# Gated cross-attention with RMS norm: the next quad's scores behind the last attention products of the quad before

## The chip, the cores and the metric

One core of a Trainium2 chip runs the kernel. The metric is the time of one execution on the device in microseconds (us), as the median of several runs. Five engines work side by side, each through its own queue: TensorE (PE in the profile, its weight loads PEld), VectorE (DVE), ScalarE (ACT), GpSimd (POOL) and SyncE (SP), which here only issues DMAs.

## The reference

```python
memory_proj = einsum('bme,de->bmd', memory, W_mem)
scores = einsum('bnd,bmd->bnm', hidden_states, memory_proj) / sqrt(D)
attn = softmax(scores, axis=-1)
memory_context = einsum('bnm,bmd->bnd', attn, memory_proj)
gate_input = concatenate([hidden_states, memory_context], axis=-1)
gate = sigmoid(einsum('bnf,df->bnd', gate_input, W_gate) + b_gate)
fused = hidden_states + gate * memory_context
return fused * rsqrt(mean(fused ** 2, axis=-1) + 1e-6) * norm_w
```

hidden_states (x) is 8 x 1024 x 1024, memory is 8 x 64 x 512, W_mem is 1024 x 512, W_gate is 1024 x 2048, all in float32.

## The kernel before

**Preparation.** Up to some 84 us the kernel projects the memory, multiplies the projection with the second half of W_gate, so that the context's part of the gate becomes attn times a small matrix (mg), and prepares sums of the blocks of W_gate's first half. Then come 16 **quads** of 512 rows of x, two to a batch (QPB is 2).

**The gate's large product.** Each quad multiplies x (512 x 1024) with the first half of W_gate (1024 x 1024) by Strassen's method in Winograd's form, on two levels. The outer level has seven products, done in the order 1, 6, 7, 5, 4, 2, 3 (ORDER, line 527). Their left sides are the transposed blocks of x (tiles a11, a12, a21, a22) and outer sums of these, S1 to S4 (outer_s, line 254; S3 overwrites a21 and S4 uses S2 and a12). Each outer product is again split into seven small ones, which the code names A, B, C, D, A again, E, F (outer_product, line 669): two matmuls each, 128x256 out, in float32, which the profile shows as four matmul records. Their left sides are quarters of the outer left side or the inner sums s1 to s4 (inner_s, line 283), which GpSimd makes in two parts: s1 and s2 first, then s3 and s4. B uses s2, C uses s3, D uses s1, F uses s4. A to F land in PSUM banks of which there are five; VectorE adds them up (u2, u3, u4 and the sums in fin), and GpSimd adds u's into the output tiles ahead of that (pre).

**The order of work** is written out by hand. Every small product is one **slot**; a quad has 49, and t0 is its first. at(slot, fn) places an operation just before the small product of that slot, mid((q, o), fn) places it in outer product o of quad q, between the second A and E. plan(q), line 530, fills both for one quad. All engines take what is queued in program order.

**Attention.** In slot 7 (before A of product 6) scores(q) multiplies the transposed x with the projected memory: 16 matmuls (k = 0..7, r = 0, 1), 64 columns wide, so that two run side by side in halves of the array (128*64 in the profile), into psT; ScalarE copies it to sT (line 309). Slot 9 transposes it on TensorE (sc), slots 10 and 13 do the softmax on VectorE and ScalarE, slot 18 transposes the result (pa, line 342), ScalarE copies it to attnT. Outer products 5, 4, 2 and 3 then carry attention's products between the second A and E: eight matmuls of 64 rows, again two side by side (64*128), half of them into pc (the context), half into the banks A, F, E, D (the gate's second part).

**x.** load_xq(q + 1) in slot 2 loads the next quad's x into a single buffer; transpose_x makes the blocks of A on VectorE, 128x512 at a time: rows 2 and 3 beside products 5 and 2, rows 0 and 1 in slots 36, 38, 43 and 45. Outer sums 1 and 2 of the next quad stand beside product 3, outer sums 3 and 4 in slot 7. Outer sum 3 overwrites a21, which scores reads.

**mg and the bias.** For a new batch load_mg loads mg in slot 49, which is slot 0 of the next quad, once attention's products of product 3 have read the old one. add_bias (line 371) then adds b_gate to its second half by an accumulating DMA on GpSimd's queue, in slot 8.

**Behind the gate.** sigmoid on ScalarE, gated on VectorE (times pc), the residual x by an accumulating DMA on GpSimd's queue, square on ScalarE and norm on VectorE, which for the second half of a quad's rows fall into slots 3 to 14 of the next quad.

Of the kernel before, what the change touches and what calls it, by code (L numbers as in the profile page):

```python
# [20 lines left out]
def tile_gated_cross_attention_rmsnorm(  # L21
# [46 lines left out]
    QPB = N // QT  # L68
# [31 lines left out]
    def t4k(pool, shape, tag, name):  # L100
        return pool.tile(shape, F32, tag=tag, name=name)
# [33 lines left out]
    for k in range(KD):  # L135
        t = t4k(*((gpool, [P, D], "gate") if k < 7 else (apool, [P, D], "s4")), f"w2_{k}")
# [383 lines left out]
    def at(slot, fn, *args):  # L520
        due.setdefault(slot, []).append(lambda: fn(*args))

    def mid(key, fn, *args):
        beside.setdefault(key, []).append(lambda: fn(*args))
# [5 lines left out]
    def plan(q):  # L530
        t0 = SLOTS * q
        nxt = q + 1 < NQ
        order = [o for o, _ in ORDER]
        for i, o in enumerate(order):
            for part, t in ((0, 1), (1, 5)):
                if i + 1 < len(order):
                    at(t0 + 7 * i + t, inner_s, q, order[i + 1], part)
                elif nxt:
                    at(t0 + 7 * i + t, inner_s, q + 1, order[0], part)
        at(t0 + 7, scores, q)  # L540
        at(t0 + 7, outer_s, q, 3)
        at(t0 + 7, outer_s, q, 4)
        at(t0 + 9, transpose_scores, q)
        at(t0 + 10, softmax_a, q)
        at(t0 + 13, softmax_b, q)
        at(t0 + 18, transpose_attn, q)
        at(t0 + 21, attn_difference, q)
        if not nxt:
            at(t0 + 5, load_last)
            return  # L550
        at(t0 + 2, load_xq, q + 1)
        for t in (2, 3):
            mid((q, 5), transpose_x, q + 1, t, 0)
            mid((q, 2), transpose_x, q + 1, t, 1)
        for i, t, half in ((36, 0, 0), (38, 1, 0), (43, 0, 1), (45, 1, 1)):
            at(t0 + i, transpose_x, q + 1, t, half)
        mid((q, 3), outer_s, q + 1, 1)
        mid((q, 3), outer_s, q + 1, 2)
        if (q + 1) % QPB == 0:
            at(t0 + 10, load_mp, (q + 1) // QPB)  # L560
            at(t0 + 49, load_mg, (q + 1) // QPB)
        if q % QPB == 0:
            at(t0 + 8, add_bias, q // QPB)

    for o in (2, 3):
        w1_place(o)
# [246 lines left out]
    for q in range(NQ):  # L813
        plan(q)
        for o, ext in ORDER:
            outer_product(q, o, ext)
# [29 lines left out]
```

## Time and profile before

| | |
|---|---|
| median of 3 runs | 980.95 us (980.92 to 981.3) |
| profiled span | 979.4 us |
| granted TensorE clock, mean | 0.996 |
| TensorE busy | 964.8 us |
| VectorE busy | 820.4 us |
| GpSimd busy | 730.5 us |
| ScalarE busy | 324.9 us |
| scores (psT), 16 blocks of 32 matmul records | 58.8 us |
| start of the scores in quads 7 and 8 | 421.00 and 476.05 us |

How to read the lines that follow: a row of the timeline holds the start in us, the duration in us, the engine, the line of the code, the operation, "written<-read" by the program's names with buffer numbers left out, the shape, and how many instructions were merged. In brackets stands how long the engine was idle just before, and what released it. Matmuls are pipelined, so their durations overlap: what counts is the distance from one start to the next. A row of the waits has engine and operation, what it waited for, the sum in us, how often and the longest. "issue" is time in which the engine waited for nothing that the profile shows. Names: kA to kF are the small products, u and gate are VectorE's and GpSimd's sums of them, l is the tile of inner sums, a and s are the left sides.

### The profile page before, as it was taken

What the parts mean: (1) busy time and instruction counts of PE and PEld (TensorE: products, weight loads), DVE (VectorE), ACT (ScalarE), POOL (GpSimd) and SP (SyncE); (2) the same over time, 40 slices, a digit from 0 to 9 for tenths busy, and PEclk for the clock granted to TensorE, in tenths of its full rate; (3) what the DMA queues carried; (4) which work ended last, traced back from release to release, by engine and by line L of the source; (5) the groups of instructions that cost most, each with busy time, mean ns of one, the idle gap of its engine ahead of it and who ended that gap; (6) DMA issues with size and microseconds to landing.
All of it is one profiled execution on the core that took longest, in us unless ns stands there. A gap on an engine that the chain in (4) does not pass through costs nothing.

```text
span 979.4 us, 14277 instructions
## 1 busy us (share of the span) xinstructions
PE 964.8 (99%) x4938; PEld 769.8 (79%) x4938; DVE 820.4 (84%) x1487; ACT 324.9 (33%) x602; POOL 730.5 (75%) x881
## 2 busy tenths in 40 slices
PE   9999999999999999999999999999999999999995
PEld 6546888888887888888887888888887888888873
DVE  3888788979797988979797988979797988979787
ACT  1100234151433334151433334151433334151434
POOL 3366877878787877878787877878787877878772
PEclk9999999999999999999999999999999999999998
DMA  9865264482918374482918374482818364482612
GB/s 372 258 153 145 39 120 107 103 188 62 186 65 165 108 141 106 102 190 65 183 65 164 111 138 105 107 184 66 182 65 168 110 136 104 108 184 68 169 65 86
DMA packets 71255, 128.32 MB, mean 131 GB/s; under 512 B 12432, under 2 KB 49296, under 8 KB 70928
## 3 DMA queue, kind: packets, MB, share of 16 engines
q1 hardware_dynamic: 61760, 93.34, 35.3%
q0 software_dynamic: 9280, 33.56, 18.5%
q8 instruction: 39, 0.64, 0.3%
q10 hardware_dynamic: 144, 0.52, 0.2%
q14 instruction: 32, 0.26, 0.1%
HBM read 87.56 MB, written 39.85 MB: 130 GB/s over the span
## 4 chain that ended last, share of the span: by engine, by line
PE 96%; DVE 2%; DMA 1%; issue 0%; ACT 0%; POOL 0%; DVEq 0%; ACTq 0%
PE kA L92 20%; PE pc L92 12%; PE kE L92 11%; PE kF L92 10%; PE kD L92 10%; PE kC L92 10%; PE kB L92 10%; PE psT L92 6%; PE pg L92 5%; PE pm L92 3%; DVE gate L95 1%; DMA memq<-in_mem 1%; DVE gate L660 0%; PE pa L342 0%; PE sc L316 0%
## 5 line engine op out<-in xcount | busy, mean ns | idle before, releaser
L95 POOL TENSOR_TENSOR gate<-gate,u 128x256 f32<-128x256 f32 x336 | 270.4, 835 | 115.7 <-DVE u L95 110.1
L582 ACT ACTIVATE gate<-gate 128x512 f32<-128x512 f32 x128 | 79.0, 629 | 400.1 <-DVE gate L95 400.1
L95 POOL TENSOR_TENSOR l<-a 128x256 f32<-128x256 f32 x128 | 128.9, 1007 | 60.4 <-DVE a L95 55.8
L248 DVE STREAM_TRANSPOSE a<-xq 128x512 f32<-128x512 f32 x128 | 137.9, 1098 | 4.0 <-DMA xq<-in_x 4.0
L92 PE MATMUL pc<-mg,attnT 64*128 64x256 f32 x512 | 127.4, 389 | 0.0
L611 DVE SCALAR_TENSOR_TENSOR gate<-gate,ss,nw_sb 128x512 f32<-128x512 f32 x120 | 126.0, 1060 | 1.1
L92 PE MATMUL kD<-it,l 128*128 128x256 f32 x448 | 115.0, 379 | 0.0
L92 PE MATMUL kB<-it,l 128*128 128x256 f32 x448 | 115.0, 379 | 0.0
L92 PEld LDWEIGHTS pc<-mg,attnT 64*128 64x128 f32 x512 | 90.6, 186 | 29.7 <-issue 21.2
L92 PE MATMUL kA<-w,a 128*128 128x256 f32 x384 | 98.7, 379 | 0.4 <-ACT u L726 0.4
L92 PEld LDWEIGHTS kD<-it,l 128*128 128x128 f32 x448 | 85.1, 190 | 11.6
L92 PEld LDWEIGHTS kB<-it,l 128*128 128x128 f32 x448 | 85.1, 190 | 11.6
L95 DVE TENSOR_TENSOR gate<-gate,pc 128x512 f32<-128x512 f32 x128 | 87.0, 680 | 5.8 <-ACT gate L582 5.8
L95 POOL TENSOR_TENSOR l<-s 128x256 f32<-128x256 f32 x96 | 75.7, 789 | 10.8 <-PE kF L92 10.7
L92 PEld LDWEIGHTS kA<-w,a 128*128 128x128 f32 x384 | 71.6, 190 | 10.2 <-ACT u L726 0.8
L726 ACT COPY u<-kA 128x256 f32<-128x256 f32 x112 | 40.5, 362 | 102.1 <-PE kA L92 99.9
L92 PE MATMUL kE<-it,a 128*128 128x256 f32 x256 | 69.0, 392 | 0.0
L95 DVE TENSOR_TENSOR u<-u,kB 128x256 f32<-128x256 f32 x112 | 45.5, 406 | 28.1 <-PE kB L92 24.9
L92 PE MATMUL kA<-t,s 128*128 128x256 f32 x256 | 67.4, 386 | 0.0
L92 PE MATMUL kC<-w,l 128*128 128x256 f32 x256 | 65.7, 379 | 0.0
L92 PE MATMUL kF<-w,l 128*128 128x256 f32 x256 | 65.7, 379 | 0.0
L596 ACT ACTIVATE junk<-gate 128x1024 f32<-128x1024 f32 x60 | 63.5, 1059 | 2.1 <-DMA gate<-in_x 1.2
(123 smaller groups left out, 1996.6 us busy)
## 6 DMA issues: line engine op xcount, KB each, us to landing
xq<-in_x SPq DMA_DIRECT2D x64, 512.0 KB, 9.6
gate<-in_x POOLq DMA_DIRECT2D x60, 512.0 KB, 7.8
out<-gate SPq DMA_DIRECT2D x60, 512.0 KB, 2.6
w<-in_w_gate_t SPq DMA_DIRECT2D x8, 512.0 KB, 11.0
w<-in_w_gate_t SPq DMA_DIRECT2D x2, 2048.0 KB, 15.6
mg<-mgd SPq DMA_DIRECT2D x16, 256.0 KB, 4.0
mpd<-mpT SPq DMA_DIRECT2D x4, 512.0 KB, 3.8
mgd<-mpq SPq DMA_DIRECT2D x16, 128.0 KB, 2.6
```

Of the source, the lines that this page charges most:

```text
L92: pin(nc.tensor.matmul(o, lhsT, rhs, start=start, stop=stop, skip_group_check=True))
L95: pin(eng.tensor_tensor(o, a, b, op))
L248: nc.vector.transpose(A[key][:, :, r * P : (r + 1) * P], chunks(xq[q][:, 4 * t : 4 * t + 4, :], KD)[:, half * KH : (half + 1) * KH],)
L582: pin(nc.scalar.activation(g, g, AF.Sigmoid))
L596: nc.scalar.activation(junk, O[q, t], AF.Square, accum_out=ss[:, t % 2 : t % 2 + 1])
L611: nc.vector.scalar_tensor_tensor(g[:, cols], g[:, cols], rstd[:, t % 2 : t % 2 + 1], nw_sb[:, cols], ALU.mult, ALU.mult,)
L726: pin(nc.scalar.copy(p1, kb["A"]))
```

## The change

Three things move; no operation is added or taken away.

1. scores(q + 1) is done at the end of quad q, beside product 3, directly behind its attention products and ahead of E, instead of in slot 7 of its own quad. Only quad 0 keeps its scores in slot 7. Attention's products and the scores, both done in parts of the array, so follow each other, and the scores' wait is out of the way of outer sum 3, which overwrites a21.
2. The last two transpositions of the next x are in slots 42 and 43 instead of 43 and 45, so that all of x is there when the scores begin.
3. The bias's DMA stands in slot 4, the fifth product of the quad, instead of slot 8; again quad 0 keeps its place.

```diff
-        at(t0 + 7, scores, q)
+        if q == 0:
+            at(t0 + 7, scores, q)
         at(t0 + 7, outer_s, q, 3)
         at(t0 + 7, outer_s, q, 4)
...
         for t in (2, 3):
             mid((q, 5), transpose_x, q + 1, t, 0)
             mid((q, 2), transpose_x, q + 1, t, 1)
-        for i, t, half in ((36, 0, 0), (38, 1, 0), (43, 0, 1), (45, 1, 1)):
+        for i, t, half in ((36, 0, 0), (38, 1, 0), (42, 0, 1), (43, 1, 1)):
             at(t0 + i, transpose_x, q + 1, t, half)
+        mid((q, 3), scores, q + 1)
         mid((q, 3), outer_s, q + 1, 1)
         mid((q, 3), outer_s, q + 1, 2)
...
         if q % QPB == 0:
-            at(t0 + 8, add_bias, q // QPB)
+            at(t0 + (4 if q else 8), add_bias, q // QPB)
```

## The prediction

> **What bounds the kernel now.** I read the page's busy line and its chain first.
>
> ```profile
> PE 964.8 (99%) x4938; PEld 769.8 (79%) x4938; DVE 820.4 (84%) x1487; ACT 324.9 (33%) x602; POOL 730.5 (75%) x881
> PE 96%; DVE 2%; DMA 1%; issue 0%; ACT 0%; POOL 0%; DVEq 0%; ACTq 0%
> ```
>
> TensorE has matmuls in flight 99% of the span and the chain lies on it for 96%. So the time falls only if TensorE gets less to do, and it rises as soon as TensorE waits. The granted clock is 0.996. Next I read one quad (the eighth) in order of time. A product slot is four matmul records and takes 0.86 us (474.23 to 475.09). Around the scores, TensorE shows:
>
> ```profile
> 474.23 1.03 PE L92 MATMUL kE<-it,a 128*128 128x256 f32 x4
> 475.09 1.03 PE L92 MATMUL kF<-w,l 128*128 128x256 f32 x4
> 476.05 3.67 PE L92 MATMUL psT<-a,mpb 128*64 128x256 f32 x32
> 479.65 1.13 PE L92 MATMUL kA<-t,s 128*128 128x256 f32 x4
> 480.62 1.03 PE L92 MATMUL kB<-it,l 128*128 128x256 f32 x4
> ```
>
> Without the scores, kF to kB would be two slots, 1.73 us; it is 5.53 us, so the scores' block costs **3.80 us**: 16 pairs at 0.216 us (0.86/4) are 3.46 us, and 0.34 us goes at its two edges. The waits of the weight loads show the same edges: psT's first load waits 5.3 us in 16 times, the first load of E behind attention's products 21.2 us in 64 times, 0.33 us each, with nothing released by another engine.
>
> Then VectorE (DVE) over the same stretch, down to product 7's u:
>
> ```profile
> 476.15 0.42 DVE L95 TENSOR_TENSOR gate<-u,kF 128x256 f32<-128x256 f32 x1 [0.44 <-PE kF L92]
> 478.04 1.23 DVE L95 TENSOR_TENSOR a<-a,a 128x1024 f32<-128x1024 f32 x1 [1.47 <-PE psT L92]
> 479.18 1.22 DVE L95 TENSOR_TENSOR s<-a,s 128x1024 f32<-128x1024 f32 x1
> 481.75 0.42 DVE L95 TENSOR_TENSOR u<-u,kB 128x256 f32<-128x256 f32 x1 [1.35 <-PE kB L92]
> 482.14 0.17 DVE L607 RECIPROCAL ss<-ss 128x2 f32<-128x2 f32 x1
> 482.34 0.75 DVE L611 SCALAR_TENSOR_TENSOR gate<-gate,ss,nw_sb 128x512 f32<-128x512 f32 x1
> ...
> 489.96 0.41 DVE L95 TENSOR_TENSOR u<-u,kB 128x256 f32<-128x256 f32 x1
> 490.48 0.42 DVE L95 TENSOR_TENSOR u<-u,kC 128x256 f32<-128x256 f32 x1
> ```
>
> DVE idles 1.47 and 1.35 us while TensorE does the scores; from 481.75 to 490.48 no row carries a wait: softmax, four norm passes of the quad before and product 6's sums fill it. Who waits for that last u is in the rows of GpSimd (POOL) and of the weight loads:
>
> ```profile
> 491.03 2.10 POOL L95 TENSOR_TENSOR gate<-gate,u 128x256 f32<-128x256 f32 x3 [1.54 <-DVE u L95]
> 493.09 0.73 POOL L95 TENSOR_TENSOR l<-s 128x256 f32<-128x256 f32 x1
> ```
> ```profile
> 492.93 0.84 PEld L92 LDWEIGHTS kB<-it,l 128*128 128x128 f32 x4
> 493.87 0.77 PEld L92 LDWEIGHTS kC<-t,l 128*128 128x128 f32 x4
> ```
>
> GpSimd starts product 7's three additions when u arrives, then makes s3 of product 5 (l<-s), finished at 493.82. TensorE's C of product 5 loads exactly that tile at 493.87, where the 0.86 cadence from 492.93 gives 493.79. Its matmul still starts on cadence (494.01 in the timeline, 0.86 behind B). The load is already held by 0.08 us, and the next microsecond of lateness lands on TensorE. So there is **a second chain without slack**: F of product 1, DVE, GpSimd, C of product 5. The quad before has 0.04 us (s3 ends at 438.71, the load is at 438.77, its cadence at 438.75).
>
> **What the Trainium skill says.** TensorEngine Tiling (Array Packing), Tiling Modes, Key Properties: changing the tiling mode drains TensorE. The trace agrees: about 0.2 us at each edge. TensorE: Matmul & The Clock Gate, "Architectural detail", says VectorE and ScalarE take instructions strictly in order; the DVE rows agree, since the outer sums behind a late instruction never overtake it. SBUF — State Buffer, "Who interferes with whom", says a VectorE instruction with two SBUF inputs and a GpSimd instruction that reads SBUF exclude each other. The trace agrees: the norm pass takes 0.75 us with GpSimd idle (482.34) and 1.05 and 1.23 us beside its additions, and the l<-a beside the second outer sum takes 1.64 us instead of 0.73.
>
> **The change part by part.**
>
> *Scores behind attention's products of product 3.* The 512 matmul records stay. Fifteen of sixteen scores blocks move. Attention's products of a product show: A to first pc 0.96 us (465.19 to 466.15), first pc to E 1.93 (to 468.08) against 8 pairs at 0.216 = 1.73, E to F 0.97. So their edges cost 0.10 + 0.20 + 0.10 = 0.40 us, the scores' 0.34; four edges, 0.74. Afterwards three are left, since the step from 64*128 to 128*64 is one edge. No row shows this step; at the least it costs an ordinary edge, 0.15 to 0.2 us (saving 0.2), at most two (saving nothing). I take 0.2, since each of the four known edges costs about that: **-0.2 us a quad**.
>
> *What the scores did where they stood.* They lay between F of product 1 and B of product 6 and gave the second chain 3.80 us, of which DVE idled 1.47 + 1.35 = 2.82. Taking them away leaves 0.98 us missing. A busy DVE starts the next instruction some 0.08 us before the recorded end of the last (u<-u,kB at 490.48 is an exception, it reads the one before; the outer sum at 479.18 begins at 478.04 + 1.14), twice: 0.98 - 0.16 = 0.82. In steps: F's sum starts 1.06 behind kF's start; + 0.34 (the spacing of sums back to back, 485.44 to 485.77 in the timeline), + 1.14, + 1.14 (the two outer sums) puts product 6's first u at 3.68 behind kF, 1.95 behind kB's start (1.73); in the profile it is 1.13. The difference is 0.82. Everything from there to product 7's u is back to back, so it is later by this against TensorE; GpSimd has 1.54 us of idle before that u, so it passes it on; s3 of product 5 is later by it, and C's load has no slack. On the way, D's bank of product 6 (free 0.76 us ahead of B of product 7) and the softmax result (0.63 us ahead of the transposition pa, quad median) come late too, by 0.1 to 0.3 us, but this is contained in the same shift, not added to it. New contention: the norm pass at 482.34, alone now, meets GpSimd's second sum for product 7: 0.07 us if DVE comes first, up to 0.7 if it waits for the whole GpSimd instruction. I take 0.08 and keep the ends. **+0.9 us a quad** (0.8 to 1.5), for the 15 quads from the second on.
>
> *x's last transposes at slots 42 and 43 instead of 43 and 45.* Same instructions. F of product 2 is summed at 462.01, so the two (1.10 us each) with a gating between end near 465.05 instead of 466.31; the scores begin at 468, so TensorE does not wait for them. Product 3's first u and the GpSimd additions behind it come 1 us later, but TensorE now spends 3.6 us on scores before E, and GpSimd's next tile (s3 of product 1, ready at 470.1) is read 1.5 + 3.6 us later. Hidden, 0. The next x load follows the last transpose and starts 1.3 us sooner; it is first read some 30 slots later: 0.
>
> *The copy of psT on ScalarE* now stands ahead of product 3's sigmoids, which wait for E and F, later on TensorE: 0. *Outer sums 1 and 2 and product 3's sums* on DVE lie beside the scores: 0, as TensorE did not wait for them before.
>
> *Bias DMA at slot 4* (7 quads). It waits on GpSimd's queue for mg's load, issued when attention's products end (413.17) and landing 4.0 us after issue. GpSimd comes to it around 418, and behind it stand the residual DMAs and product 6's s3, wanted near 426 on the delayed TensorE: 0. At slot 8 it took 0.83 us and 0.94 of idle in the stretch that is now short, where it would have cost, so the move avoids a loss rather than gains.
>
> Sum: 15 x (0.9 - 0.2) = 10.5 us, **991.5 us**.
>
> **Rivals.** (a) *The DVE shift is absorbed*, because s3 of product 5 can be reached sooner than I think, and the edges alone count: 15 x -0.2 = -3, 978.0. For it: TensorE hardly waits today and DVE is 84% busy on average. Against: 0.04 to 0.08 us between tile and load. (b) *Half is absorbed*, as the spread of norm passes (0.75 to 1.23 us) comes out better in the new order: stall 0.2 to 0.5, 981 to 985.5. (c) *Contention doubles it*: stall over 1.4, past 999, near 1002.
>
> **Numbers.** Forecast 0.70, (a) 0.13, (b) 0.12, (c) 0.05. The range takes the forecast's stalls of 0.6 to 1.4 us (987 to 999) and the upper two thirds of (b). Faster by over 0.2% (under 979.0) is (a) with the edge saved: 0.12. Within 0.2% is (a) without the saving and the lowest third of (b): 0.05. Slower: 0.83.
>
> **What would show it.** psT directly behind the pc rows, E 3.6 us later, one 0.33 us weight-load wait fewer a quad; no DVE wait on psT; product 6's first u without a wait on kB; new waits of PE or PEld in front of kC of product 5 on GpSimd's l, perhaps in front of pa and kB of product 7 on DVE, about 0.9 us a quad; quads of 55.75 instead of 55.05 us (the spacing of the scores' starts, 421.00 to 476.05). I am wrong if quads last 54.85 and kC keeps its cadence, or if the waits stand elsewhere, as in front of the scores.

## The result, and the profile after

The changed kernel takes 992.59 us (median of 4 runs, 991.76 to 993.23) against 981.0 us before (four runs; the table above has three of them): ratio 1.0117, 95% interval 1.01 to 1.0135. It is **11.6 us slower**. The prediction was 991.5 us, with stalls that would give 987 to 999 us.

First the page's chain of the changed kernel, shares of the span by engine:

```profile
PE 75%; DVE 14%; issue 4%; POOL 3%; DMA 2%; ACT 1%; DVEq 0%; POOLq 0%; ACTq 0%
```

TensorE's part fell from 96% to 75%: the chain now leaves it, mostly for VectorE and GpSimd. TensorE's timeline in the same quad as before, the eighth:

```profile
471.63 0.38 PE L92 MATMUL pc<-mg,attnT 64*128 64x256 f32 x1
...
471.95 3.67 PE L92 MATMUL psT<-a,mpb 128*64 128x256 f32 x32
475.55 1.13 PE L92 MATMUL kE<-it,s 128*128 128x256 f32 x4
476.52 1.03 PE L92 MATMUL kF<-w,l 128*128 128x256 f32 x4
...
482.56 1.03 PE L92 MATMUL kF<-w,l 128*128 128x256 f32 x4
483.43 1.03 PE L92 MATMUL kA<-t,s 128*128 128x256 f32 x4
484.29 1.03 PE L92 MATMUL kB<-it,l 128*128 128x256 f32 x4
...
497.24 1.03 PE L92 MATMUL kB<-it,l 128*128 128x256 f32 x4
498.35 1.13 PE L92 MATMUL kC<-t,l 128*128 128x256 f32 x4
499.32 1.03 PE L92 MATMUL kD<-it,l 128*128 128x256 f32 x4
```

psT follows attention's last pc after 0.32 us, as any first matmul behind an edge does (0.216 and 0.10), and E follows psT after 3.60 us, as A did before. There is one edge less, and F to B is 1.73 us. But B to C of product 5 is 1.11 us and C to D 0.97, where the cadence is 0.86. VectorE, GpSimd and the weight loads say why:

```profile
483.63 0.42 DVE L95 TENSOR_TENSOR gate<-u,kF 128x256 f32<-128x256 f32 x1 [0.44 <-PE kF L92]
483.96 1.22 DVE L95 TENSOR_TENSOR a<-a,a 128x1024 f32<-128x1024 f32 x1
485.10 1.22 DVE L95 TENSOR_TENSOR s<-a,s 128x1024 f32<-128x1024 f32 x1
486.24 0.41 DVE L95 TENSOR_TENSOR u<-u,kB 128x256 f32<-128x256 f32 x1
486.57 0.16 DVE L609 RECIPROCAL ss<-ss 128x2 f32<-128x2 f32 x1
486.76 0.75 DVE L613 SCALAR_TENSOR_TENSOR gate<-gate,ss,nw_sb 128x512 f32<-128x512 f32 x1
```
```profile
486.98 1.12 POOL L95 TENSOR_TENSOR l<-l,a 128x256 f32<-128x256 f32 x1
...
495.52 2.10 POOL L95 TENSOR_TENSOR gate<-gate,u 128x256 f32<-128x256 f32 x3 [1.54 <-DVE u L95]
497.58 0.71 POOL L95 TENSOR_TENSOR l<-s 128x256 f32<-128x256 f32 x1
```
```profile
490.73 0.73 PEld L92 LDWEIGHTS kB<-it,l 128*128 128x128 f32 x4 [0.41 <-DVE gate L95]
493.50 0.20 PEld L342 LDWEIGHTS pa<-ident,e 128*128 128x128 f32 x2 [0.32 <-issue]
498.35 0.73 PEld L92 LDWEIGHTS kC<-t,l 128*128 128x128 f32 x4 [0.49 <-POOL l L95]
```

Both idle spans of VectorE are gone. Product 6's first u starts 1.95 us behind B's start (486.24 - 484.29), before 1.13. s3 of product 5 ends at 497.58 + 0.71 = 498.29, and C loads at 498.35. Start to start, TensorE loses 0.29 us around B of product 7, 0.12 at pa and 0.36 around C of product 5, 0.77 in all; every quad from the second on shows the three. The waits of the whole run have one group more that matters:

```profile
PEld kC L92 <- POOL l L95: 8.7, 20, 0.5
PEld kB L92 <- DVE gate L95: 6.3, 15, 0.4
PEld kA L92 <- ACT u L728: 5.5, 8, 1.5
ACT junk L598 <- DMA gate<-in_x: 23.4, 8, 4.3
```

The last two (before: 2.8 us in three times and 1.2 in two) are a second loss. ScalarE's squares wait about 3 us for the residual's DMA in the quads of a new batch. Before, the residual's second half landed 16.2 to 18.3 us after the start of such a quad, and the squares stood at 17.4 us; now it lands at 16.3 to 18.0 us, and the squares stand at 13.6, since the scores' 3.8 us no longer lie ahead of them. ScalarE's copy of product 5's first result stands behind them, and the second A of product 5 waits for that copy. From the starts of the scores, a quad lasts 55.63 us in most cases (before 55.05), and 55.88, 55.94, 55.93, 56.98 and 56.07 in five of the seven new-batch quads. The account: 15 x 0.58 = 8.7 us for the first loss, net of the edge; 0.25 + 0.31 + 0.30 + 1.35 + 0.44 = 2.65 for the second; 11.35 together, and the spans differ by 11.3 (990.7 and 979.4).

### The profile page after: what moved, and what is told of

Same layout as the page of the kernel before. It is cut to its first block, busy times and chain, and to the rows that moved or that the text cites. A ratio compares the mean times of both kernels' runs of the same rounds, so it can differ in the third digit from the quotient of the medians.

```text
span 990.7 us, 14301 instructions
## 1 busy us (share of the span) xinstructions
PE 973.8 (98%) x4938; PEld 766.6 (77%) x4938; DVE 823.4 (83%) x1487; ACT 327.1 (33%) x602; POOL 733.3 (74%) x881
## 4 chain that ended last, share of the span: by engine, by line
PE 75%; DVE 14%; issue 4%; POOL 3%; DMA 2%; ACT 1%; DVEq 0%; POOLq 0%; ACTq 0%
PE kA L92 13%; PE pc L92 12%; PE kE L92 9%; PE kC L92 8%; PE kF L92 7%; PE kD L92 7%; PE kB L92 6%; PE psT L92 6%; PE pg L92 5%; DVE gate L95 4%; DVE gate L613 4%; PE pm L92 3%; DVE u L95 3%; POOL gate L95 2%; DMA gate<-in_x 1%
## 5 line engine op out<-in xcount | busy, mean ns | idle before, releaser
L95 POOL TENSOR_TENSOR gate<-gate,u 128x256 f32<-128x256 f32 x336 | 284.9, 878 | 114.9 <-DVE u L95 110.2
L95 POOL TENSOR_TENSOR l<-a 128x256 f32<-128x256 f32 x128 | 116.4, 909 | 37.5 <-PE kB L92 32.9
L92 PEld LDWEIGHTS kD<-it,l 128*128 128x128 f32 x448 | 85.1, 190 | 11.6
L95 DVE TENSOR_TENSOR gate<-gate,kE 128x256 f32<-128x256 f32 x112 | 45.4, 417 | 46.9 <-PE kE L92 41.3
L95 DVE TENSOR_TENSOR gate<-gate,kF 128x256 f32<-128x256 f32 x112 | 45.5, 418 | 25.3 <-PE kF L92 20.1
```

The lines of the kernel that those rows point to most:

```text
L92: pin(nc.tensor.matmul(o, lhsT, rhs, start=start, stop=stop, skip_group_check=True))
L95: pin(eng.tensor_tensor(o, a, b, op))
```

## The experiments

All times are medians; in brackets behind them stand the ratio to the kernel before, measured beside them at 980.86 to 980.91 us, and its 95% interval.

**e1: outer sum 3 beside the scores.** On the changed kernel:

```diff
-        at(t0 + 7, outer_s, q, 3)
+        if q == 0:
+            at(t0 + 7, outer_s, q, 3)
...
         mid((q, 3), outer_s, q + 1, 2)
+        mid((q, 3), outer_s, q + 1, 3)
```

> Outer sum 3 of the next quad moves from slot 7 to the stretch beside the scores (behind outer sums 1 and 2), where VectorE waits 2.42 us for E in the profile after. Theory (a chain VectorE, GpSimd, C of product 5 without slack): product 6's first u starts where TensorE's B ends again, about 1.1 us behind B's start instead of 1.95, the waits in front of B of product 7 (0.29 us with its edge), pa (0.12) and C of product 5 (0.36) are gone, quads last about 54.85 us, and the time falls to 978 to 981 us (one edge less a quad, 15 x 0.2 = 3 us under the kernel before; what ScalarE waits for the residual's DMA in new batches may take back up to 3). Rival (the scores in their new place cost by themselves, by the step between the two divisions of the array or by contention): about 992 us, as after.

Measured 988.0 us (1.0068, 1.0055 to 1.0082), outside both expectations. The trace separates two kinds of quads. Those without a new batch last 54.85 us (359.12 to 413.97 by the scores' starts), exactly one edge under 55.05, without a wait in the three places, and product 6's first u is back at 1.13 us behind B: the theory holds there. The new-batch quads lose more than in the changed kernel:

```profile
PEld kA L92 <- ACT u L730: 11.1, 10, 2.4
ACT junk L600 <- DMA gate<-in_x: 24.0, 7, 5.3
```

With the first loss gone, the squares come up sooner and wait 3.4 us on average, and up to 4.7 us of a quad reach TensorE. e3 and e4, planned together with e1, and e5, e9 and e10 behind it ask what makes the residual late.

**e2: one norm pass less in the packed stretch.** On the changed kernel, when = (17, 18, 23, 25, 26, 33) instead of 28 at the end.

> In the changed kernel the last of the four norm passes of the quad before moves from slot 14 to slot 19, out of the packed stretch on VectorE (0.81 us from start to start). The outer sums stay. Theory (work on VectorE up to product 7's u): the wait of C of product 5 (0.36 us) goes, those of B of product 7 and pa, which lie ahead of slot 14, stay (0.41): 15 x 0.36 = 5.4 us, about 987 us. Rival (GpSimd's later start behind outer sum 3 is what counts, not VectorE's queue): no change, 992.6 us.

Measured 988.63 us (1.0078, 1.0065 to 1.0091), 4.0 less than the changed kernel. B of product 7 and pa still wait, and C of product 5 keeps the cadence: its wait is VectorE's lateness passed on, and GpSimd's later start alone does not make it. Ordinary quads last 55.27 us (137.51 to 192.78 by the scores' starts), 0.36 less than 55.63. Of the 5.4 us expected, the rest is lost again in the new-batch quads, whose second loss grows from 2.65 to 3.8 us, as in e1.

**e3: the bias in slot 8 again.** On the changed kernel, at(t0 + 8, add_bias, ...) as before.

> The changed kernel with the bias's DMA back in slot 8. Theory: in slot 8 it stands on GpSimd between the inner sums and the additions of the stretch without slack, where it took 0.83 us and 0.94 of idle before: 0.3 to 0.5 us more for each of the seven quads, 995 to 996 us, and ScalarE's squares go on waiting about 3 us for the residual in these quads, because the stretch before them is 3.8 us shorter. Rival (the bias in slot 4, ahead of the residuals in the queue, makes the residual late): the squares' waits go, and with them the extra of some 2.5 us: 990 to 993 us.

Measured 1022.41 us (1.0421, 1.0407 to 1.0435): both expectations are far off. Every new-batch quad loses 4.7 us against the others, most of it in front of B of product 7, the rest at its C and D. VectorE and GpSimd in one of them:

```profile
441.67 0.41 DVE L95 TENSOR_TENSOR u<-u,kD 128x256 f32<-128x256 f32 x1
442.00 4.67 DVE L613 SCALAR_TENSOR_TENSOR gate<-gate,ss,nw_sb 128x512 f32<-128x512 f32 x1
446.60 0.41 DVE L95 TENSOR_TENSOR gate<-gate,kA 128x256 f32<-128x256 f32 x1
```
```profile
441.17 0.82 POOL L372 DMA_DIRECT2D mg<-in_b_gate  x1
441.74 2.36 POOL L95 TENSOR_TENSOR gate<-gate,u 128x256 f32<-128x256 f32 x3
443.80 0.97 POOL L95 TENSOR_TENSOR l<-a 128x256 f32<-128x256 f32 x1
444.48 0.97 POOL L95 TENSOR_TENSOR l<-a,l 128x256 f32<-128x256 f32 x1
445.16 0.96 POOL L95 TENSOR_TENSOR l<-s 128x256 f32<-128x256 f32 x1
446.19 1.07 POOL L95 TENSOR_TENSOR l<-l,s 128x256 f32<-128x256 f32 x1
```

A norm pass that takes 0.75 us alone and 0.9 to 1.25 beside GpSimd takes 4.67 us here: it ends 0.55 us after the sixth of the instructions that GpSimd, coming straight from the bias's DMA issue, runs without a gap (446.12; the seventh follows after 0.07 us). So the place of the bias decides about far more than its own 0.83 us. The squares still wait 14.3 us in seven times, with the bias behind the residuals: so without the bias ahead of them about 2 us each remain.

**e4: the bias's move alone.** On the kernel before, slot 4 instead of 8.

> The kernel before with the bias's DMA in slot 4, nothing else changed. Theory (its place costs nothing): 981 us within 0.1%, squares wait for the residual at most 1 us. Rival (the bias ahead of the residuals makes them late): squares wait 1 to 3 us in the seven quads of a new batch, and the time rises by up to 3 us.

Measured 982.89 us (1.002, 1.0011 to 1.0028). The squares wait 15.8 us in seven times (before 1.2 in two), and four quads pass some of it on, the most 1.2 us. The rival is right: with the bias ahead of the residuals the squares wait about 2 us also without the rest of the change. Together the two give about 3 us (changed kernel, e1), less than their sum.

**e5: e1 with the bias in slot 5**, queued behind the residuals and product 6's inner sums: at(t0 + (5 if q else 8), add_bias, ...).

> Outer sum 3 beside the scores as in e1, and the bias's DMA in slot 5, where it is queued behind the residual's DMAs and product 6's inner sums but ahead of the crowded stretch. In e1 the quads without a new batch lasted 54.85 us, the others up to 4.7 us more, where ScalarE's squares waited 3.4 us for the residual. Theory (the bias ahead of the residuals makes up about half of this wait): the waits fall to about 2 us, ScalarE's copy for product 5 comes in time in most quads, and the time is 978 to 981 us. Rival (the wait comes from the shorter stretch and x's load alone): as e1, 986 to 989 us.

Measured **978.95 us** (0.9981, 0.9973 to 0.9989), under both kernels. The waits that answer to those of e1:

```profile
ACT junk L600 <- DMA gate<-in_x: 13.3, 7, 2.4
PEld kA L92 <- ACT u L730: 2.8, 3, 1.5
```

The squares wait 1.9 us each, and this no longer reaches TensorE: the 2.8 us of kA on ScalarE are those that the kernel before has too.

**e6: e5 with the scores apart from attention's products.** at(t0 + 46, scores, q + 1) in place of mid((q, 3), scores, q + 1).

> As e5, but the scores in slot 46, ahead of product 3's second A, so that a full-size product lies between them and attention's products. Nothing is saved at the edges then. Theory (each edge between divisions of the array costs about 0.2 us, and joining the two saves one): 0.2 us more a quad than e5, 15 x 0.2 = 3 us more than e5, quads of 55.05 us. Rival (the joint placement saves nothing): the same time as e5.

Measured 998.07 us (1.0176, 1.0162 to 1.0191). As a total it answers nothing, since all seven new-batch quads wait 1.3 to 2.4 us in front of B of product 5, where VectorE and GpSimd wait for output tiles that are still being stored (21.3 and 13.2 us in seven times each). The other quads answer it: 55.05 us (134.69 to 189.73) against 54.85 in e5. An edge is worth 0.20 us.

**e7 and e8: outer sum 4 twice, and three times, on the kernel before.**

```diff
-            tt(nc.vector, s, a12, S[q, 2], ALU.subtract)
+            for _ in range(2):   # e8: 3
+                tt(nc.vector, s, a12, S[q, 2], ALU.subtract)
```

> The kernel before with outer sum 4 done twice in slot 7 (1.14 us more on VectorE, the same values written again). Theory (behind outer sum 4 VectorE idles 1.35 us until product 6's B, and only what exceeds this reaches TensorE): no change, 981 us. Rival (VectorE is short of time over the whole quad): some 1 us a quad, 995 us and more.

> The kernel before with outer sum 4 done three times (2.28 us more on VectorE). Theory (the chain over VectorE and GpSimd to C of product 5 passes on what exceeds the idle 1.35 us): product 6's first u comes 0.85 to 0.95 us later, and TensorE waits about 0.8 us a quad in front of B of product 7, pa and C of product 5, as in the changed kernel: 992 to 995 us. Rival (this chain has slack): 981 us, as with the sum twice.

e7: 985.83 us (1.0054, 1.0042 to 1.0067), between the two expectations. The quads from the second on last 55.17 us, 0.12 more; 2.85 us more come from the first quad, where one VectorE sum takes 3.71 us beside GpSimd, behind the bias's DMA issue as in e3. e8: 1010.31 us (1.03, 1.0285 to 1.0314), quads of 56.84. It is more than expected, because the repeated sums, too, share with GpSimd:

```profile
434.98 4.55 DVE L95 TENSOR_TENSOR s<-a,s 128x1024 f32<-128x1024 f32 x3
439.45 0.41 DVE L95 TENSOR_TENSOR u<-u,kB 128x256 f32<-128x256 f32 x1
```

Three take 4.55 us instead of 3 x 1.14. But the relation that they were to test comes out, with the delay of product 6's first u behind B's start taken from each trace:

| kernel | first u behind B, us | later than before | TensorE's stall a quad |
|---|---|---|---|
| before | 1.13 | 0 | 0 |
| e7 | 1.37 | 0.24 | 0.12 |
| changed | 1.95 | 0.82 | 0.78 (55.63 - 55.05 + 0.20) |
| e8 | 3.04 | 1.91 | 1.79 |

What exceeds about 0.1 us reaches TensorE in full in these four kernels.

**e9: the changed kernel with the bias in slot 5.**

> The changed kernel (outer sum 3 back in slot 7) with the bias's DMA in slot 5, behind the residuals. Theory (two separate losses: the chain over VectorE and GpSimd, 0.58 us net in each of 15 quads, and the residual's lateness in the new batches, some 2.5 us in all, of which the bias ahead of it makes the part that reaches TensorE): only the second goes, 15 x 0.58 = 8.7 us over the kernel before, 989.5 to 990.5 us. Rival (the bias's place does not matter while the chain is late): 992.6 us.

Measured 989.66 us (1.0089, 1.0076 to 1.0103). All quads from the second to the fifteenth stall alike now, and 992.59 - 989.66 = 2.9 us is what the bias's place costs in the changed kernel.

**e10: e5 with x's load ahead of mg's.** at(t0 + 48, load_xq, q + 2) in place of load_xq(q + 1) in slot 2.

> As e5, with the load of the quad after next placed in slot 48, ahead of mg's load on SyncE's queue. In a new batch it no longer waits for attention's products of product 3 and mg's issue, and starts about 3 us sooner, as in the other quads. Theory (the residual is late because it shares the DMA engines with x's 2 MB): the squares' wait falls from 1.9 us on average to under 1 us, and what is left of the new-batch quads' excess (0.02 to 0.4 us) goes: 978 us, up to 1 us below e5. Rival (mg, now behind x, lands late and holds the bias on GpSimd's queue): slower than e5 by 1 us or more.

Measured 995.13 us (1.014, 1.012 to 1.016; its five runs spread from 991.19 to 997.43): the rival. The squares hardly wait (3.8 us in seven times): in each of the seven new-batch quads the residuals land 0.7 to 1.7 us sooner than in e5, though issued at the same point of the quad. So x's load beside them did make them late. But mg now lands 13.5 us after issue (median) instead of 3.8 in e5, and the bias holds GpSimd's queue until then (the first two rows; that one of them also reads 13.5, a sum of three waits, is chance):

```profile
POOL mg L372 <- issue: 18.0, 4, 4.9
POOL mg L372 <- DMA mg<-mgd: 13.5, 3, 4.9
PEld kC L92 <- POOL l L95: 9.3, 7, 1.3
PEld kB L92 <- DVE gate L95: 7.9, 7, 1.5
```

**e11: x's last transposes in slots 42 and 43 alone**, on the kernel before.

> The kernel before with x's last transposes in slots 42 and 43, nothing else changed. Theory (hidden): 981 us within 0.1%. Rival (product 3's u, 1 us later, makes s3 of product 1 late, which has 1.5 us): up to 0.5 us a quad, 985 to 988 us.

Measured 980.92 us (1.0, 0.9992 to 1.0009): hidden. The squares wait a little more, 5.1 us in six times instead of 1.2 in two; every quad still lasts 55.05 us.

## Why the prediction was right, and where it was not

- **The edge, -0.2 us a quad: right.** 0.20 in e5 against e6, and in e1's ordinary quads (54.85).
- **The chain F of product 1, VectorE, GpSimd, C of product 5: right.** Its steps gave 1.95 us for the first u behind B; the trace has 1.95. The forecast waits stand at B of product 7, pa and C of product 5 and nowhere else on this chain. e1 and e5 remove it by taking an outer sum out, e2 takes a part out at another place, e7 and e8 lengthen it.
- **The stall of 0.9 us: mis-sized, 0.78** (quads of 55.63 us instead of 55.75). The term for contention (0.08) was nothing: VectorE's norm pass takes 0.75 us at 486.76 as before, and GpSimd's sum waits (1.12 instead of 0.73). And some hundredths of slack were left: in e7 0.24 us of lateness cost 0.12. In 15 quads this is 1.8 us too much.
- **"Behind it stand the residual DMAs ...: 0": wrong.** The step looked at when GpSimd's next sums are needed, not at when the residuals land, nor at who waits for them. Before, the squares waited 1.2 us in all, but in the new-batch quads the residual landed at best 1.3 us ahead of them; the change without the bias's move (e3) and the bias's move alone (e4) each make the squares wait about 2 us. In the changed kernel 2.65 us of it arrive at TensorE, by way of ScalarE's copy for product 5. Putting the bias one slot later is enough to keep them off (e9).
- The two errors, -1.8 and +2.65, nearly cancel; the closeness of the total (10.5 forecast, 11.6 measured) owes something to that.
- **"At slot 8 it would have cost": right in sign, far too small.** 4.7 us a quad instead of the 0.83 and 0.94 us named (e3).
- **Transposes, the copy of psT, outer sums 1 and 2: 0, right** for the transposes (e11); for the others the trace shows no wait of TensorE beside the scores, but they were not tried alone.

## What to carry to other kernels

A block of work on the bounding engine is also time for all the others: before moving it, ask which idle of theirs it made possible, add up what is queued behind that idle, and follow it to the next tile that the bounding engine reads. An engine that hardly ever waits can have a chain beside it that arrives with less than 0.1 us to spare; compare when a tile ends with when its weight load begins. When such a move costs, take the work that lost its shelter along: one outer sum of 1.14 us moved beside the scores, and a DMA one slot later, turned 11.6 us of loss into 2 us of gain.

## What the runs showed of the hardware

A VectorE instruction with two inputs in SBUF can wait through a whole series of GpSimd instructions, not only through one. Beside GpSimd's additions a norm pass usually takes 0.9 to 1.25 us; among GpSimd rows that follow a DMA issue on its queue without a gap, it took 4.67 to 4.81 us (e3, in every new-batch quad) and a 128x512 sum 3.71 (e7, once), each until some 0.55 us after GpSimd's sixth instruction. The Trainium skill (SBUF — State Buffer, "SBUF: two separate sides") says that whichever of the two starts first gets the shared ports for the whole instruction; these stretches show that the other can also miss its turn between the instructions of a series. Where an idle stretch of 0.30 to 1.97 us followed the bias's issue (the kernel before, e7 and e8, in their new-batch quads), it did not happen. But the unbroken series alone is not the cause: in the first quad of the kernel before, GpSimd goes on without a gap behind the bias's issue too (97.03 us), and VectorE's sums of two inputs there take 0.83 to 1.24 us. What decides between the two stays open.
